# A graph attention layer: two conversions and a set of tables placed later in the prologue, and the last two steps and six pairs written out in a new order

## The chip, the cores and the metric

The kernel runs on one core of one Trainium2 chip. The time is device microseconds (us) of one execution. A core has engines that run their own instruction streams side by side: PE (matrix multiplies and transposes), DVE (vector work), ACT (scalar engine: copies, exponentials, gelu, square roots), POOL (GpSimd) and SP, which here only issues transfers. PEld in a profile is the loading of weights into PE. SBUF is the memory beside the engines, PSUM the small memory into which PE writes.

## The reference

One layer of graph attention with 12,500 nodes of 256 numbers, 8 heads of 32, and 200,000 edges, sorted by their destination `dst`:

```python
h = maximum(layernorm(x), 0)                       # 12500 x 256
q, k, v = h @ Wq + bq, h @ Wk + bk, h @ Wv + bv    # 8 heads of 32
logits = einsum(q[dst], k[src]) / sqrt(32)         # per edge and head
expv = exp(logits - segment_max(logits, dst)[dst])
attn = expv / segment_sum(expv, dst)[dst]
agg = segment_sum(attn * v[src], dst)              # per node
out = gelu(agg + h @ Wskip + bskip)
y = h + out
return x + layernorm(y) * gamma + beta
```

So each edge fetches a row of k and v of its source node, meets the q of its destination node, and is added into that node.

## The kernel before, in words

**Prologue.** `project()` (L156 to L279) walks the nodes in 98 blocks of 128, in groups of 1, 2, 4, then sixteen of 5, then 4, 4, 2 and 1. Per group `prepare` loads x (SP), takes the statistics (DVE L211 to L222) and writes h (ACT L226). Per block PE transposes h (L140), multiplies it by the weights of k and v (L257, three PSUM buffers `ps_kv`) and of q (L263, one PSUM buffer `ps_q`). DVE evicts both with their biases (kvo L260, qp L267); ACT L268 and POOL L269 split q into two parts. SP stores h, k and v, and q into tables in DRAM (`h_tab`, `kv_tab`, `q_pc`).

`make_plan` (L422 on) shares the prologue with it: it makes from the edge list what the walk needs. It loads dst and src (POOL), writes them out shifted (`dst_p`, `src_p`), gathers from these 66 rows per stream by 16 indirect transfers on POOL (`dch`, `sch`, L488), converts them to floats on DVE (`sf` L492, `df` L507), sends the first destinations through DRAM into one row (`d_d` L518, `d_row` L519; in the code they are called d0_d and d0_row), copies these (L523, L524, L552), transposes `sf` on PE (L496) into the gather indices `idx`, and ends with the tables `e_tab` (POOL L667) and a flag (L700). `make_near` (L703 to L758) makes tables of bands from POOL's masks: `near_m` L711 is written by POOL, DVE makes `near_p`, `near_s` (L740), `near_g`. In `project` it is called at group 4, and the small tables of biases (`pieces`, L112), gamma, the skip weights and a block of zeros for `q_pc` at group 3.

The order of instructions on each engine in this part is chosen by a scheduler that follows the dependencies and the order of the code. `behind` adds a dependency without a semaphore, which pins an instruction after another in the order of its engine. So a DVE conversion may stand ahead of the eviction of a later block, and then that eviction starts after it.

**Walk.** `walk_streams` (L760 on) cuts the edges into 8 streams and walks them in NST = 66 steps of 384 edges per stream, in 3 tiles of 128 (K = 3; the last step has 2). Per step POOL gathers 24 tiles of k and v by indirect DMA (L1035); PE spreads q over the edges (L1075), DVE multiplies (`times` L1084) and sums over the heads' elements (`total` L1091), PE turns the logits (`turn` L1099), DVE scans for running maxima (`maxima` L1110, L1111), ACT takes exponentials (L1117), PE turns the weights back (`turn_back` L1126), DVE weighs the values (`weigh` L1139), PE adds them up by node (`add_up` L1165), ACT copies the sums (L1177, L1183), and SP stores them into a table of partial sums (L1187). Here `keep` (L778) pins every instruction behind the one before on its engine: the order of calls in the code is the order on each engine.

**Pairs.** When all edges of two blocks of nodes are done, a `Pair` (L809) finishes them: `fetch` (sums, x and h by SP, L837), `divisors`, `divide` (L842 to L856, DVE), `turn` (transposes L850, copy hT on ACT L853), `skip` (h by the skip weights, L863, L867) and `add` (L872) on PE, `gelu` (ACT L876), `stats` (L879 to L885), `root` (ACT L889), `factors` (L893, L894), `normal` (ACT L899), `shifted` (x plus beta on PE, L906, L909), `scale` (L913, L915), `store` (SP L920). The function `table_of` (L987) loads an ACT table where the next function needs another. In the loop three pairs are in flight, called pair, before and older. The last four pairs are of the class `Last` (L923), which keeps its tiles in a half of a gathered k and v tile that is free.

**The end.** The loop runs to step 64; in its last round it takes in the pairs that are left. Step 65, its pair and the four `Last` pairs are then written out after the loop (the part from `c = NST - 1` on). Stores to `out` are at addresses known only at run time, and each waits for the one before.

Of the kernel before, what the change touches and what calls it, by code (L numbers as in the profile page):

```python
# [36 lines left out]
SP = mybir.EngineType.SP  # L37
DVE = mybir.EngineType.DVE
# [3 lines left out]
P = 128  # L42
# [28 lines left out]
def gnn_kernel(ctx: ExitStack, tc: tile.TileContext, x, src, dst, Wq, bq, Wk, bk, Wv, bv,  # L71
# [84 lines left out]
    def project():  # L156


        last, turned, products = None, None, []
# [9 lines left out]
        with tc.tile_pool(name="proj_c", bufs=1) as cpool, \  # L169
# [63 lines left out]
            for g, (b0, n) in enumerate(zip(starts, sizes)):  # L233
# [3 lines left out]
                if g == 4:  # L237
                    make_near(tc, near, near_n, lambda ins: behind(ins, last))
                if g == 3:
# [13 lines left out]
                for b in range(n):  # L253
# [13 lines left out]
                    nc.vector.tensor_tensor(q, ps_q, b_q, op=OP.add)  # L267
# [11 lines left out]
        return products  # L279
# [62 lines left out]
    with tc.tile_pool(name="pln", bufs=1) as pool, tc.tile_pool(name="pln_e", bufs=1) as ep, \  # L342
            tc.tile_pool(name="pln_ps", bufs=1, space=PSUM) as psum:
        products = project()
        make_plan(tc, pool, ep, psum, src, dst, N, LEN, NST, SLACK, NT, dram, ident, flag,
                  idx, d0_row, slot_row, e_tab, pen_tab, products, 4 * HID, 4 * KV)
# [75 lines left out]
def make_plan(tc, pool, ep, psum, src, dst, N, LEN, NST, SLACK, NT, dram, ident, flag, idx, d0_row,  # L422
              slot_row, e_tab, pen_tab, products, bytes_x, bytes_row):
# [6 lines left out]
    C = -(-max(E, (S - 1) * LEN + SLACK + STEP * NST + 1) // P)  # L430
    dst_p = dram.tile([1 + P * C, 1], I32, name="dst_p")
# [60 lines left out]
    nc.vector.tensor_copy(sf[:, :, :CH], sch)  # L492
# [14 lines left out]
    nc.vector.tensor_copy(df[:, :, :CH], dch[:, :, :CH])  # L507
# [15 lines left out]
    nc.vector.tensor_copy(line[:, 0, :], d0_row[:, :S])  # L523
    nc.vector.tensor_copy(line[:, 1, :], d0_row[:, (NST - 1) * S:])  # L524
# [27 lines left out]
    nc.vector.tensor_copy(done[:, :F - S], d0_row[:, S:])  # L552
# [207 lines left out]
def walk_streams(tc, N, HID, NST, KL, many, ident, idx, d0_row, slot_row, near, near_n, e_tab, pen_tab, h_tab,  # L760
# [26 lines left out]
    def loaded(a, most):  # L787

        return nc.values_load_multi_w_load_instructions(
            a, engines=[SP], min_val=0, max_val=most,  # L790
# [18 lines left out]
    class Pair:  # L809
# [36 lines left out]
        def turn(self):  # L846
# [5 lines left out]
            self.hT = self.pool.tile([P, 2, KC, P], F32, name="hT", bufs=1)  # L852
            self.keep(nc.scalar.copy(self.hT, ps))  # L853

# [67 lines left out]

    class Last(Pair):  # L923

        own, depth = "_l", 4

        def __init__(self, pool, m, room, ps_h, ps_o, keep):
            Pair.__init__(self, pool, m, ps_h, ps_o, keep)
            self.room = room
# [23 lines left out]
    with ExitStack() as es:  # L953
# [193 lines left out]

        def add_up(c, i, tiles=range(K)):

            add_up_products(c, i, tiles)  # L1150
            if tiles[-1] == tiles_of(c) - 1:
                add_up_results(c, i)

        def add_up_products(c, i, tiles=range(K)):
            g = step[c]
            streams = [s for s in range(S) if where(s)[0] == i]
            if tiles[0] == 0:
# [4 lines left out]
            for j in tiles:  # L1162
                for s in streams:
# [3 lines left out]
                                          g["vw"][j][:, s, :], start=j == 0,  # L1167
                                          stop=j == tiles_of(c) - 1, skip_group_check=True))

        def add_up_results(c, i):  # L1170
# [3 lines left out]
            if i == 0:  # L1174
                g["sums"] = work.tile([P, 3, SUMS], F32, name="sums_w", bufs=1)
# [47 lines left out]
        assert len(rest) <= 4  # L1223
        lasts, banks = [], {}

        def room(i):
            if i % 2 == 0:
                room.tile = rows[NST % 2][i // 2].rearrange("p s d -> p (s d)")
            half = S * KV // 2
            return room.tile[:, i % 2 * half:i % 2 * half + half]  # L1230

        def bank(i):
            def get():
                if i % 2 == 0:
                    banks[i // 2] = qe_ps.tile([P, 2, 2, HID], F32, name="ps_qe")
                return banks[i // 2][:, i % 2]
            return get

        def last(i):
            if i < len(rest):  # L1240
                lasts.append(Last(fin, rest[i], room(i),
                                  lambda: hot_ps.tile([P, 2, KC, P], F32, name="ps_hot"),
                                  bank(i), keep))
                lasts[i].fetch_rows()

        pair = before = older = None
        for c in range(NST - 1):
# [82 lines left out]
            if c == NST - 2:  # L1330
                if before:
                    before.shifted()
                    before.scale()
                    before.store(0)
                    before.store(1)
                if pair_next:
                    pair_next.fetch()
                for i in range(4):
                    last(i)
# [8 lines left out]
            if c == NST - 2:  # L1348
                weigh(c, K - 1)
                add_up(c, 0, range(K - 1, K))  # L1350
                add_up(c, 1)
                if pair_next:
                    pair_next.turn()
                    pair_next.skip()
            if c == NST - 2:
                add_up(c, 2)
            older, before, pair = before if c < NST - 2 else None, pair, pair_next
# [3 lines left out]
        c = NST - 1  # L1361
        for j in range(tiles_of(c)):
            if tiles_of(c) == K and j < 2:
                times(c, K - 1, j)
            hot_n(c, j)
            if tiles_of(c) == K and j == 1:
                total(c, K - 1)
        if tiles_of(c) == K:
            turn(c, K - 1)
        maxima(c)  # L1370
        exponent(c)
        if before:
            before.stats()
        if pair:
            pair.divisors()
            pair.divide()
        turn_back(c)
        carried(c)
        if before:
            before.root()  # L1380
# [413 lines left out]
```

## Time and profile before

| | us |
|---|---|
| median of 3 runs | 2448.26 |
| lowest, highest | 2444.04, 2455.95 |
| the profiled execution | 2449.12 |
| its span, from the first to the last instruction | 2447.3 |
| PE busy | 1708.7 (70%) |
| DVE busy | 1999.8 (82%) |
| ACT busy | 1066.4 (44%) |
| POOL busy | 1658.1 (68%) |
| first gather of the walk | 359.12 |
| last gather of the walk | 2360.52 |

Some 1.8 us of the profiled execution lie outside its span. The granted clock of PE has a mean of 0.737 of full speed. Busy shares are means over the whole span. In a row of a group, "x1576 | 1521.3, 965 | 482.4" means 1576 instructions, 1521.3 us of busy time, 965 ns for one, and 482.4 us in which the engine stood idle just before them; behind the arrow stands what ended the wait. In a row of a timeline the first number is the start from the beginning of the span, the second the duration, and the bracket the idle time before it.

### The profile page before, as it was taken

How to read it: one execution, taken by the hardware profiler on the slowest of the kernel's cores; microseconds unless marked ns; L12 is line 12 of the kernel's file. 1: busy time of each engine (PE TensorE's matmuls, PEld its weight loads, DVE VectorE, ACT ScalarE, POOL GpSimd, SP SyncE). 2: the span in 40 equal slices, each digit the busy share in tenths (PEclk: the TensorE clock that was granted, in tenths of full speed). 3: DMA queues.
4: the chain of work that ended last, by engine and by line, in shares of the span. 5: the costliest groups of instructions: out<-in, count | busy, mean ns of one | idle time of the engine just before them, and what ended most of it. 6: DMA issues, size and time to landing. Idle time of an engine off the chain costs nothing.

```text
span 2447.3 us, 29473 instructions
## 1 busy us (share of the span) xinstructions
PE 1708.7 (70%) x7824; PEld 909.6 (37%) x7824; DVE 1999.8 (82%) x2461; ACT 1066.4 (44%) x2328; POOL 1658.1 (68%) x1745
## 2 busy tenths in 40 slices
PE   6879983555557767767777767676676777677765
PEld 3445542222223333333333334333333343343333
DVE  7866856777778898898888888888888988888884
ACT  3333321333334544554545444445444444445443
POOL 4342447777777777777777777777777777777740
PEclk9999995666667777776667676677677767767678
DMA  7656668888888988888888988899889888889862
GB/s 259 253 207 264 251 250 263 256 255 254 255 268 266 286 276 282 285 277 284 279 285 279 287 271 282 274 285 288 275 282 287 282 281 284 277 279 287 279 202 76
DMA packets 306128, 649.33 MB, mean 265 GB/s; under 512 B 52836, under 2 KB 192238, under 8 KB 300954
## 3 DMA queue, kind: packets, MB, share of 16 engines
q0 software_dynamic: 128768, 423.23, 55.7%
q1 hardware_dynamic: 176434, 223.46, 27.2%
q8 instruction: 64, 1.05, 0.2%
q10 hardware_dynamic: 748, 0.66, 0.1%
q14 instruction: 114, 0.93, 0.1%
HBM read 538.91 MB, written 108.23 MB: 264 GB/s over the span
## 4 chain that ended last, share of the span: by engine, by line
DMA 25%; PE 23%; DVE 19%; issue 12%; POOL 10%; ACT 8%; SPq 3%; DVEq 0%; another core or an unknown queue 0%; ACTq 0%; POOLq 0%
DMA kv<-kv_tab,idx 16%; POOL kv L1035 9%; PE ps_kv L257 5%; DVE kv L1084 5%; DMA h<-h_tab 4%; PE ps_a L867 4%; DVE vw L1139 3%; DVE L L1091 3%; PE ps_qe L1075 3%; PE ps_q L263 3%; PE ps_a L1165 2%; ACT L987 2%; PE ps_hot L909 2%; DMA out_dram<-o 2%; SPq L837 2%
## 5 line engine op out<-in xcount | busy, mean ns | idle before, releaser
L1035 POOL DMA_INDIRECT kv<-kv_tab,idx x1576 | 1521.3, 965 | 482.4 <-issue 342.6
L1084 DVE TENSOR_TENSOR kv<-ps_qe,kv 128x1024 f32<-128x1024 f32 x394 | 468.8, 1218 | 191.1 <-DMA kv<-kv_tab,idx 117.9
L1139 DVE TENSOR_TENSOR vw<-ps_x,kv 128x2048 f32<-128x2048 f32 x197 | 449.4, 2281 | 9.1 <-PE ps_x L1126 9.1
L1091 DVE TENSOR_REDUCE L<-kv 128x64 f32<-128x2048 f32 x197 | 450.4, 2286 | 6.9 <-DMA et<-e_tab 0.2
L1075 PE MATMUL ps_qe<-qw,to_e 64*128 64x256 f32 (+1 forms) x1576 | 312.6, 396 | 107.5 <-DVE kv L1084 102.6
L1054 ACT ACTIVATE to_e<-ps_hot,ones 128x384 fp32r<-128x384 f32 x396 | 210.4, 573 | 316.1 <-PE ps_hot L1052 308.0
L1075 PEld LDWEIGHTS ps_qe<-qw,to_e 64*128 64x128 f32 (+1 forms) x1576 | 223.8, 248 | 272.7 <-DVE kv L1084 168.4
L1165 PE MATMUL ps_a<-vw,to_n 128*32 128x264 f32 (+1 forms) x2344 | 280.3, 516 | 4.2 <-DVE vw L1146 3.7
L1177 ACT COPY sums_w<-ps_a 128x264 f32<-128x264 f32 x130 | 49.2, 378 | 498.3 <-PE ps_a L1165 439.7
L1099 PE MATMUL ps_x<-ident,L 128*64 128x128 f32 x197 | 73.1, 371 | 274.0 <-DVE vw L1146 205.2
L1052 PE MATMUL ps_hot<-et,near 48*128 48x384 bf16 x396 | 142.5, 420 | 136.5 <-ACT to_e L1054 131.8
L257 PE MATMUL ps_kv<-w_kv,hT 128*128 128x512 f32 x392 | 194.8, 619 | 15.3 <-ACT hT L142 14.2
L269 POOL TENSOR_TENSOR qp<-qp 128x256 fp32r<-128x256 f32 x98 | 88.4, 903 | 171.8 <-ACT qp L268 171.6
L867 PE MATMUL ps_a<-w_s,hT 128*128 128x256 f32 x368 | 171.9, 648 | 21.2 <-ACT hT L853 18.0
L1165 PEld LDWEIGHTS ps_a<-vw,to_n 128*32 128x32 f32 (+1 forms) x2344 | 99.3, 139 | 216.2 <-issue 174.4
L1099 PEld LDWEIGHTS ps_x<-ident,L 128*64 128x64 f32 x197 | 25.7, 130 | 362.7 <-DVE vw L1146 288.3
L1165 PE MATMUL ps_hot<-vw,to_n 128*64 128x264 f32 x808 | 144.8, 509 | 1.9 <-DVE o L915 1.1
L1183 ACT COPY kv<-ps_a 1x264 f32<-1x264 f32 x388 | 142.9, 368 | 6.3
L867 PEld LDWEIGHTS ps_a<-w_s,hT 128*128 128x128 f32 x368 | 115.6, 329 | 69.0 <-ACT hT L853 44.1
L987 ACT ACT_TABLE_LOAD x102 | 130.9, 1283 | 1.7
L1065 ACT ACTIVATE to_n<-ps_hot,ones 128x384 f32<-128x384 f32 x197 | 103.6, 578 | 53.7 <-PE ps_hot L1063 51.8
L263 PE MATMUL ps_q<-w_q,hT 128*128 128x256 f32 x392 | 106.1, 395 | 24.3 <-DVE qp L267 24.2
(278 smaller groups left out, 2103.2 us busy)
## 6 DMA issues: line engine op xcount, KB each, us to landing
qw<-q_pc SPq DMA_DIRECT2D x264, 128.0 KB
kv<-kv_tab,idx POOLq DMA_INDIRECT x1576
kv_tab<-kvo SPq DMA_DIRECT2D x16, 1280.0 KB
q_pc<-qp SPq DMA_DIRECT2D x16, 1280.0 KB
qw<-q_pc SPq DMA_DIRECT2D x264, 64.0 KB
table<-sums_w SPq DMA_DIRECT2D x264, 61.9 KB
pen<-pen_tab SPq DMA_DIRECT2D x66, 192.5 KB
sums<-table SPq DMA_DIRECT2D x92, 132.0 KB
```

The lines of the kernel that those rows point to most:

```text
L257: ins = nc.tensor.matmul(ps_kv, hT[:, c, :], w_kv[:, c, :], start=c == 0, stop=c == KC - 1)
L263: ins = nc.tensor.matmul(ps_q, hT[:, c, :], w_q[:, c, :], start=c == 0, stop=c == KC - 1)
L867: self.keep(nc.tensor.matmul(self.ps[:, b, :], self.hT[:, b, c, :], w_s[:, c, :], start=False, stop=False, skip_group_check=True))
L987: keep(nc.scalar.activation(dummy[:, 1:2], dummy[:, 0:1], function))
L1035: ins = keep(nc.gpsimd.indirect_dma_start(out=t[:, s, :], out_offset=None, in_=kv_tab[:, :], in_offset=bass.IndirectOffsetOnAxis(ap=idx[:, ...
L1054: keep(nc.scalar.activation(step[c]["to_e"][:, i, :], ps[:, :CH], AF.Relu, scale=-1.0, bias=ones))
L1075: keep(nc.tensor.matmul(ps[:, b, a, :], g["to_e"][at:at + w, i, j * P:(j + 1) * P], g["qw"][at:at + w, i, :], start=True, stop=True))
L1084: keep(nc.vector.tensor_tensor(k, g["qe", half].rearrange("p b a d -> p a b d"), k, op=OP.mult))
L1091: keep(nc.vector.tensor_reduce(g["L"][:, j, :].rearrange("p (s h) -> p s h", s=S), g["kv"][j][:, :, :HID].rearrange("p s (h d) -> p s h d" ...
L1139: keep(nc.vector.tensor_tensor(t[:, :, HEADS:].rearrange("p s (h d) -> p s h d", h=HEADS), wj[:, :, :, None].to_broadcast([P, S, HEADS, D] ...
L1165: keep(nc.tensor.matmul(ps[at:at + w, :], g["to_n"][:, j, i * P + at:i * P + at + w], g["vw"][j][:, s, :], start=j == 0, stop=j == tiles_o ...
L1183: keep(nc.scalar.copy(step[c + 1]["kv"][0][0:1, s, HID - HEADS:], ps[at:at + 1, :]))
```

## The change

There are two parts.

In the prologue, `make_near` is called at group 13 instead of 4, and the small tables, gamma, the skip weights and the zeros at group 12 instead of 3. `project` now also returns the list of evictions of q (`biased`), and `make_plan` pins `df` behind the eviction at 36% of this list, `sf` behind that at 43%, and the copies of `d0_row` behind that at 45%.

At the end, the loop stops two steps earlier than the edge list, and the steps a = 64 and b = 65 are written out together. The add-ups of these two steps take the tiles in the order 1, 0, 2 (`turns`). The sums of b are copied into a free half of a gathered tile. The pair of step 64 (`late`) becomes a `Last`, so that there are five of them, and its rows and those of the others are fetched earlier. Three pairs, before, pair and late, are finished together as `ends`; their six stores are issued by POOL (`store_aside`) instead of SP. The four last pairs follow; their turn and skip are spread among the work of the others.

```diff
-                if g == 4:
+                if g == (4 if len(sizes) < 16 else 13):
                     make_near(tc, near, near_n, lambda ins: behind(ins, last))
-                if g == 3:
+                if g == (3 if len(sizes) < 16 else 12):
                     for ins in [rows(gam, gamma)] + \
                             [weights(w_s, Wskip)]:
                         behind(ins, products[-1])
...
-                    nc.vector.tensor_tensor(q, ps_q, b_q, op=OP.add)
+                    biased.append(nc.vector.tensor_tensor(q, ps_q, b_q, op=OP.add))
...
+    def behind(ins, share):
+
+        tc.add_manual_dep(ins.ins, biased[len(biased) * share // 100].ins.name,
+                          mybir.DependencyInfo(mybir.DependencyClass.NoSync,
+                                               mybir.DependencyReason.DATA), reason="kept order")
...
-    nc.vector.tensor_copy(sf[:, :, :CH], sch)
+    behind(nc.vector.tensor_copy(sf[:, :, :CH], sch), 43)
...
-    nc.vector.tensor_copy(df[:, :, :CH], dch[:, :, :CH])
+    behind(nc.vector.tensor_copy(df[:, :, :CH], dch[:, :, :CH]), 36)
...
-    nc.vector.tensor_copy(line[:, 0, :], d0_row[:, :S])
-    nc.vector.tensor_copy(line[:, 1, :], d0_row[:, (NST - 1) * S:])
+    behind(nc.vector.tensor_copy(line[:, 0, :], d0_row[:, :S]), 45)
+    behind(nc.vector.tensor_copy(line[:, 1, :], d0_row[:, (NST - 1) * S:]), 45)
...
-    nc.vector.tensor_copy(done[:, :F - S], d0_row[:, S:])
+    behind(nc.vector.tensor_copy(done[:, :F - S], d0_row[:, S:]), 45)
...
+        def store_aside(self):
+
+            nodes = loaded(slot_row[0:1, self.m, 0:2], (N - P) * BX, POOL)
+            for b in range(2):
+                self.keep(nc.gpsimd.dma_start(at_byte(out_b, nodes[b], P, HID),
+                                              self.y[:, b, :].bitcast(U8)))
...
+        def turns(c):
+
+            return range(K) if c < NST - 2 else (1, 0, 2)[:tiles_of(c)]
...
-        for c in range(NST - 1):
+        for c in range(NST - 2):
...
+        a, b = NST - 2, NST - 1
...
+        weigh(a, 0)
+        lasts[3].fetch_rows()
+        late.turn()
+        late.skip()
+        weigh(a, 2)
+        maxima(b)
+        add_up_products(a, 0, (0,))
+        add_up_products(a, 1, (1, 0))
+        exponent(b)
+        before.stats()
+        add_up(a, 0, (2,))
+        add_up_products(a, 2, (1, 0))
+        turn_back(b)
+        add_up(a, 1, (2,))
+        add_up(a, 2, (2,))
+        carried(b)
+        for j in range(2):
+            hot_n(b, j)
+        lasts[0].turn()
+        lasts[0].skip()
+        weigh(b, 1)
+        pair.divisors()
+        pair.divide()
+        pair.add()
         for i in range(3):
-            add_up(c, i, range(tiles_of(c) - 1))
-        weigh(c, tiles_of(c) - 1)
+            add_up_products(b, i, (1,))
+        table_of(AF.Gelu)
+        pair.gelu()
+        weigh(b, 0)
         for i in range(3):
-            add_up(c, i, range(tiles_of(c) - 1, tiles_of(c)))
...
+            add_up(b, i, (0,))
         for p in lasts:
             p.fetch_sums()
...
+        late.divisors()
+        late.divide()
+        late.add()
+        late.gelu()
+        pair.stats()
+        lasts[1].turn()
+        lasts[1].skip()
+        late.stats()
+        table_of(AF.Sqrt)
+        ends = (before, pair, late)
+        for p in ends:
+            p.root()
+        for p in ends:
+            p.factors()
+        for p in ends:
+            p.normal()
+        lasts[2].turn()
+        lasts[2].skip()
+        for i, p in enumerate(ends):
+            p.shifted()
+            p.scale()
+            p.store_aside()
+            if i == 0:
+                lasts[3].turn()
+                lasts[3].skip()
+            elif i == 1:
+                lasts[0].divisors()
+                lasts[0].divide()
+                lasts[0].add()
+        table_of(AF.Gelu)
+        for i, p in enumerate(lasts):
+            if i:
+                p.divisors()
+                p.divide()
+                p.add()
             p.gelu()
         table_of(AF.Sqrt)
```

## The prediction

> **What bounds the kernel now.** I read three things in this order: the page (what is busy, and when), the busy time by stretches of the span with the waits of the first stretch, and the single instructions where a wait looked long. The page first, its rows of 40 slices of 61 us each:
>
> ```profile
> span 2447.3 us, 29473 instructions
> ...
> DVE  7866856777778898898888888888888988888884
> ...
> POOL 4342447777777777777777777777777777777740
> PEclk9999995666667777776667676677677767767678
> ...
> L1035 POOL DMA_INDIRECT kv<-kv_tab,idx x1576 | 1521.3, 965 | 482.4 <-issue 342.6
> ```
>
> PEclk and POOL change character at slice 6 and at the last one: there are three stages, and they have different limits. The table by stretches (columns: PE, PEld, DVE, ACT, POOL busy, granted clock, DMA share, GB/s) shows how much each engine has to do in each:
>
> ```profile
> 60.00:80.00 20.00, 14.31 (x45) 7.36 (x44) 17.00 (x55) 3.49 (x10) 8.24 (x13) 0.98 0.31 132
> ...
> 100.00:120.00 20.00, 19.11 (x67) 11.28 (x66) 14.44 (x51) 9.14 (x24) 9.38 (x12) 1.00 0.90 321
> 120.00:140.00 20.00, 13.75 (x42) 7.75 (x41) 11.84 (x27) 5.16 (x14) 15.22 (x15) 0.91 0.56 216
> 140.00:160.00 20.00, 13.06 (x40) 7.47 (x39) 11.17 (x37) 5.21 (x14) 6.91 (x9) 0.83 0.57 209
> ...
> 200.00:240.00 40.00, 38.71 (x149) 24.01 (x149) 22.79 (x68) 15.14 (x42) 9.56 (x14) 1.00 0.64 243
> ...
> 357.00:2360.00 2003.00, 1353.43 (x6592) 703.86 (x6592) 1695.16 (x1696) 908.28 (x1945) 1520.78 (x1576) 0.69 0.88 276
> 2360.00:2447.00 87.00, 51.30 (x223) 30.11 (x223) 44.58 (x92) 33.61 (x65) 0.52 (x1) 0.77 0.31 94
> ```
>
> *The walk*, 357 to 2360: 1576 gathers on POOL, 0.965 us each plus 0.30 of "issue" between them, so 24 a step make 30.2 us, and the scans of successive steps do start 30 us apart (2289.80, 2319.62, 2350.29). The diff adds and removes no gather. This stage stays as it is, and whatever the first stage gains moves the end by as much.
>
> *The prologue*, 0 to 357: PE is busy 38.71 of 40 us where nothing disturbs it, and two blocks then take 6.16 us, 3.08 a block. The evictions of q (L267) date the blocks: block 0 at 19.5, 6 at 45.5, 18 at 92.1, 24 at 112.1, 36 at 163.8, 72 at 276.3, 78 at 299.8, 97 at 355.2. Against 3.08 a block, blocks 6 to 18 lose 46.6 - 37.0 = 9.6 us, 18 to 24 lose 1.5, 24 to 36 lose 51.7 - 37.0 = 14.7, 36 to 72 lose 1.6, 72 to 78 lose 5. The waits of this stage (us in total, times, longest) and two conversions in the order of time say who did it:
>
> ```profile
> PE ps_q L263 <- DVE qp L267: 24.2, 13, 6.6
> ...
> DVE st L211 <- DMA x_in<-in_x_dram: 10.0, 6, 4.3
> ...
> DVE near_s L740 <- POOL near_m L711: 5.0, 4, 2.1
> ```
>
> ```profile
> 131.39 1.94 DVE L507 CAST df<-dch 66x3072 f32<-66x3072 int32 x1 [5.96 <-DMA sch<-src_p,at_i]
> ...
> 151.22 1.76 DVE L492 CAST sf<-sch 66x3072 f32<-66x3072 int32 x1 [7.94 <-DMA sch<-src_p,at_i]
> ```
>
> DVE stands before a conversion whose gather has not landed, the eviction of the only ps_q buffer stands behind it in DVE's order, and PE waits 4.05 us at 134.31 and 6.56 us at 154.61, with 1.82 at 123.83 12.4 of its 24.2. Those two stretches are the ones with 13 to 14 us of PE in 20.
>
> *The tail*, 2360 to 2447: DVE is busy half of it. Its longest wait, and SP's at the very end:
>
> ```profile
> 2391.50 2.29 DVE L1139 TENSOR_TENSOR vw<-ps_x,kv 128x2048 f32<-128x2048 f32 x1 [9.10 <-PE ps_x L1126]
> ```
>
> ```profile
> SPq L920 <- DMA out_dram<-kv: 12.3, 7, 3.2
> ```
>
> **The change, part by part.** Times below are of the profiled execution, 2449.1 us with 1.8 around its span; the median of the runs shown is 0.9 lower.
>
> *1. Conversions later.* The two programs' instruction lists put df behind the eviction of block 36 (it was 29), sf behind 51 (was 33), the d0_row copies behind 52 (was 34). The gathers themselves are issued earlier, at blocks 14 to 21 instead of 25 to 31, because what fed them stood behind the tables on DVE. That leaves 15 blocks, 46 us, between the last gather and df; before, the last one landed by 151.2, about 35 us after the first was issued. So both waits (5.96 and 7.94) go, and with them PE's 12.4. DVE's work, counted by the times of its rows from start to start, in blocks 18 to 35 falls to 6 to 10 us per six blocks, against a pace of 18.5, so nothing is late next there. I take -12; bounds -12.4 and -6 (one of the two waits only, its share being given up elsewhere).
>
> *2. Loads of x.* The wait of 4.27 at 121.45 fell when the gathers crowded the DMA engines (0.90 busy from 100 to 120). The gathers move, so the crowd moves, to blocks where DVE has slack. I take -2; bounds 0 and -5.6 (4.27 and another 1.38 at 107.3).
>
> *3. Tables later.* make_near's 71 DVE instructions leave blocks 6 to 14 for 42 to 51. They are 25.6 us of busy time (some 18 from start to start, since successive ones overlap), with 5.0 of waiting for POOL's masks (near_s). At the old place blocks 6 to 18 lost 9.6; the counted work there falls from 19.2 and 19.1 us per six blocks to 17.4 and 15.8, under the pace: gain 5, between 0 and 9.6. At the new place it rises to 17.9, 18.9 and 20.1 in blocks 42 to 59, and the 5.0 of waits comes along: excess 0.4 + 1.6 = 2.0 at least, 9.6 at most (what the same tables cost at the old place); I take +5, between 7.0 (all of the waits) and 2.0. Parts 1 and 3 meet here: sf and the plan's chain behind it now stand at the tables' heels.
>
> *4. Other queues in the prologue.* ACT's two stores of zeros and its loads of gamma and the skip weights are issued 45 blocks later; nobody reads them before the walk, over 140 us on. On POOL, d_row waited 7.87 us for d_d, queued behind the gathers (below); POOL has that slack (it waits 171.6 for ACT at L269). The transposes of sf come two blocks later. The last e_tab row was issued at 324.6, 34 us before the first gather of the walk; two blocks later (6) with the end 14 nearer leaves 14 of cover. All this at nothing; if the plan came more than 14 us later than that, the walk would wait for it.
>
> Prologue: -12 - 2 - 5 + 5 = **-14**, bounds -6 + 9.6 = +3.6 and -12.4 - 5.6 - 9.6 + 2 = -25.6.
>
> *5. The last two steps.* The same pairs, products, copies and gathers as before, in another order on every engine, and three pairs' stores on POOL's queue. What it can remove is the 9.10 above: turn_back of step 65 stood on PE behind step 64's sums and a pair's skip, and is now put ahead of the sums that DVE does not wait for. What is late next: (a) DVE comes to the last products sooner, and they need the last gather, issued at 2359.57 and landed by 2364.1 whatever the order. DVE waited 0.20 there before; I take 2 (bounds 0 and the 4.5 from issue to landing). (b) The lasts' turn and skip move between the three finishing pairs. One pair's is 3.15 us (0.45 transposes, 0.59 the copy on ACT, 2.00 matmuls, gaps). One of them with its neighbour's copy on ACT ahead of what DVE wants costs about 4 (bounds 3.15 and two, 6.3). The b sums copied at 2400.7 then come some 7 earlier, their 8 loads too, which before began at 2405.11; but the three pairs' roots, factors, normals and scales now stand ahead of the lasts' divisions and gelus, where two of them were done while the sums travelled. Sum -9.1 + 2 + 4 = **-3**; bounds -9.1 + 3.15 = -6 and -9.1 + 4.5 + 6.3 = +1.7.
>
> *6. Stores on POOL's queue.* Every store to the output waits for the landing of the one before (the 12.3 above), so six on POOL run one by one and the lasts' eight on SP wait for the sixth. Ready: DVE's last weigh ended 2396.5, less 9.1 plus 2 is 2389.4; then divide 1.1, gelu 0.6, two stats 3.3, the table 1.5, factors 1.0, three normals 3.3, scale 1.4: 2402. The lasts' first store came at 2425.54, less 3 is 2422.5. So each of the six may take 20.5 / 6 = 3.4 us. Two rows of POOL stores with a reader behind them:
>
> ```profile
> 143.07 0.61 POOL L518 DMA_DIRECT2D d_d<-d_i  x1
> ...
> 152.32 0.75 POOL L519 DMA_DIRECT2D d_row<-d_d  x1 [7.87 <-DMA d_d<-d_i]
> ...
> 176.48 0.51 POOL L579 DMA_DIRECT2D gvu_d<-gvu  x1
> ...
> 178.46 0.58 POOL L581 DMA_DIRECT2D wide<-gvu_d  x1 [0.18 <-issue]
> ```
>
> The first took 9.2 us from issue to reader, right behind gathers that landed at 151.22; the second 2.0, with nothing ahead in its queue. In the tail the queue is empty for over 35 us: 2.0, so 12 us, done at 2414 and hidden. Taking SP's own issue away is worth nothing, since SP waits for landings.
>
> A rule on this: the Trainium skill ("DMA: Bandwidth & Descriptors", Anatomy of one DMA — SWDGE) fits 2.0 us plus the bytes over 436 GB/s to a transfer issued from this engine. For 128 KB that is 2.3, an estimate from that page; six end at 2416, which leaves the sum as it is.
>
> **Sum**: 2449.1 - 14 - 3 = 2432.
>
> **The rivals.** *A: the tables only change place.* DVE is the bound in blocks 42 to 59; they lose 9.6 there, the gain at the old place is 5, only one conversion's 6 is won and nothing on x. -6 - 5 + 9.6 = -1.4, tail -3: 2445. For it: 60 to 80 shows PE at 14.31 under just this work, and three groups of 18 to 20 us in a row leave no room. Against: 200 to 240 has DVE at 22.79 of 40, half empty. *B: slower, by the stores on POOL.* Place: the six stores that the lasts' first store waits for. At 9.2 us each they take 55 and end at 2457, 34.7 behind 2422.5: 2432 + 34.7 = 2467. It decides from 3.4 us a store on, cancels all gain at 3.4 + 17/6 = 6.2 and is 12 us slower than before at 8.3. Against: the empty queue. *C: more than forecast.* Both ends of parts 1 to 3 on the good side and the whole 9.1 less 3: about 2449.1 - 25.6 - 6 = 2417. *D: it does not do what it says*: the work on DVE is the same (254 us in both, counted by the rows' times from start to start), and the gaps return at other blocks: prologue 0, tail 0, 2449.
>
> **How the numbers follow.** Half a per cent, 12 us, is about what a measurement here can tell from no change. Forecast (2427 to 2436): 0.55. C: 0.11. A: 0.22. D: 0.04. B: 0.08. Faster 0.55 + 0.11 = 0.66, same 0.26, slower 0.08. The range goes from C's end, 2416, through A to D's edge, 2448, leaving out B and a little on each side; the forecast's own is 2424 to 2437.
>
> **What would show it.** Right: df and sf without a wait, PE busy over 18 of 20 us between blocks 20 and 40, the first gather of the walk near 345 instead of 359; the 9.10 gone and a wait for the last gather of about 2 in its place; the lasts' first store waiting for DVE, not for a store on POOL. Wrong: ps_q waiting for DVE in blocks 42 to 59 for more than 7 us (A); out_dram stores on POOL over 3.4 us apart (B); a first gather at 355 or later; DVE waits on PE in the last 50 us that add up to over 9.

## The result, and the profile after

The changed kernel takes 2431.14 us (median of 6, 2427.34 to 2435.5), the kernel before 2448.48 (median of 6 beside it). The ratio is 0.9931, 95% interval 0.9917 to 0.9945: 17 us, or 0.7%, faster. The forecast was 2432.

The page of the run after, 2429.78 us long with a span of 2428.1:

```profile
span 2428.1 us, 29469 instructions
...
L1058 POOL DMA_INDIRECT kv<-kv_tab,idx x1576 | 1517.3, 963 | 482.6 <-issue 339.2
```

The gathers (now L1058) are what they were. Stage by stage, with the start of the first and of the last gather as the borders (2360.52 in the table of the kernel before is where the last one ends):

| us | before | after | difference |
|---|---|---|---|
| start to first gather | 359.1 | 338.4 | -20.8 |
| first to last gather | 2000.5 | 1996.3 | -4.2 |
| last gather to the end of the span | 87.7 | 93.4 | +5.6 |

Four later runs at this speed have 2000.4 to 2004.4 in the second line, so its 4 us are what a walk differs by from run to run. The prologue gave more than forecast (-14), and the end took time in this run where it was to give 3.

The table by stretches (PE, PEld, DVE, ACT, POOL busy, granted clock, DMA share, GB/s), the same ones as before, and one more of the prologue:

```profile
60.00:80.00 20.00, 18.81 (x64) 10.62 (x63) 16.24 (x56) 7.12 (x20) 12.28 (x14) 1.00 0.98 358
100.00:120.00 20.00, 19.01 (x64) 11.07 (x65) 10.53 (x34) 8.53 (x25) 5.08 (x7) 1.00 0.67 252
120.00:140.00 20.00, 19.11 (x67) 11.49 (x66) 11.50 (x28) 8.31 (x22) 5.13 (x6) 1.00 0.79 281
140.00:160.00 20.00, 19.11 (x64) 10.75 (x62) 16.08 (x51) 6.82 (x18) 10.35 (x10) 1.00 0.62 234
180.00:200.00 20.00, 16.98 (x59) 10.04 (x58) 20.00 (x63) 6.47 (x17) 7.57 (x8) 0.91 0.47 172
2334.00:2428.00 94.00, 60.84 (x223) 34.65 (x223) 46.08 (x97) 28.90 (x61) 4.71 (x8) 0.67 0.29 94
```

PE is busy 19 of 20 us between 100 and 160, where from 120 on it had 13 to 14. From 180 to 200, where the tables now lie, DVE is busy 20.00 of 20 and PE falls to 16.98. In the last line PE's busy time is 60.84 where it was 51.30, with the same 223 instructions and a lower clock (0.67, it was 0.77).

The two conversions in the order of time have no wait behind them, and the waits of the prologue are these (us in total, times, longest):

```profile
136.87 1.72 DVE L515 CAST df<-dch 66x3072 f32<-66x3072 int32 x1
...
191.15 1.72 DVE L500 CAST sf<-sch 66x3072 f32<-66x3072 int32 x1
```

```profile
DVE st L212 <- DMA x_in<-in_x_dram: 10.4, 8, 2.1
PE ps_q L264 <- DVE qp L268: 8.2, 8, 2.7
...
DVE near_s L748 <- POOL near_m L719: 1.7, 3, 0.9
POOL d_row L527 <- DMA d_d<-d_i: 1.6, 1, 1.6
```

PE's wait for DVE at the one buffer of q fell from 24.2 us to 8.2. The wait for x has nearly the same sum as before (10.4 for 10.0), in smaller pieces and at other blocks: in blocks 18 to 36 it fell from 5.7 us to 0.8. The end, on DVE:

```profile
2339.87 1.23 DVE L1107 TENSOR_TENSOR kv<-ps_qe,kv 128x1024 f32<-128x1024 f32 x1 [2.83 <-DMA kv<-kv_tab,idx]
...
2355.28 2.29 DVE L1162 TENSOR_TENSOR vw<-ps_x,kv 128x2048 f32<-128x2048 f32 x1 [2.69 <-PE ps_x L1149]
...
2383.24 0.69 DVE L926 TENSOR_TENSOR o<-sums,ps_hot 128x512 f32<-128x512 f32 x1 [7.84 <-PE ps_hot L920]
...
2387.78 0.69 DVE L926 TENSOR_TENSOR o<-sums,ps_hot 128x512 f32<-128x512 f32 x1 [3.25 <-PE ps_hot L920]
...
2394.27 0.69 DVE L926 TENSOR_TENSOR kv<-kv,ps_hot 128x512 f32<-128x512 f32 x1 [4.11 <-PE ps_hot L920]
```

The 9.10 before the weigh of step 65 (L1162) is 2.69. DVE waits 2.83 for the last gather. New are three waits of `scale` for the x plus beta of its pair (L920), 15.2 us together. On PE, L920 of the first pair stands behind the third last pair's skip (L878), and that skip behind a copy on ACT:

```profile
2373.59 2.07 ACT L910 ACTIVATE sums<-sums,nm,rstd 128x256 f32<-128x256 f32 x4
2375.57 1.07 ACT L910 ACTIVATE kv<-kv,nm_l,rstd_l 128x256 f32<-128x256 f32 x2
2376.55 0.56 ACT L861 COPY hT<-ps_hot 128x512 f32<-128x512 f32 x1
```

```profile
2377.16 3.78 PE L878 MATMUL ps_qe<-w_s,hT 128*128 128x256 f32 x8 [2.90 <-ACT hT L861]
```

ACT works through six normals (L910) before it copies hT; PE waits 2.90 us for it and then runs the eight products in 3.78 us, which is half clock: the trace grants 0.50 from 2377.2 to 2381, and the same eight take 1.99 elsewhere. L920 of the second pair stands behind the next skip. L920 of the third stands behind no skip, but behind the `add` of the first last pair (L883), which waits for DVE's division:

```profile
2384.37 1.99 PE L878 MATMUL ps_qe<-w_s,hT 128*128 128x256 f32 x8 [0.41 <-ACT hT L861]
...
2389.62 2.07 PE L883 MATMUL ps_qe<-kv,ident 128*128 128x256 f32 x4 [1.88 <-DVE kv L867]
...
2392.16 2.08 PE L920 MATMUL ps_hot<-kv,ident 128*128 128x256 f32 x4
```

### The profile page after: what moved, and what is told of

It reads as the page before. It is cut to its first block, busy times and chain, and to the rows that moved or that the text cites. A ratio compares the mean times of both kernels' runs of the same rounds, so it can differ in the third digit from the quotient of the medians.

```text
span 2428.1 us, 29469 instructions
## 1 busy us (share of the span) xinstructions
PE 1697.2 (70%) x7824; PEld 904.4 (37%) x7824; DVE 1996.9 (82%) x2461; ACT 1061.4 (44%) x2323; POOL 1664.4 (69%) x1751
## 4 chain that ended last, share of the span: by engine, by line
DMA 27%; PE 22%; DVE 18%; issue 12%; POOL 11%; ACT 7%; SPq 3%; DVEq 0%; another core or an unknown queue 0%; POOLq 0%; ACTq 0%
DMA kv<-kv_tab,idx 18%; POOL kv L1058 10%; PE ps_kv L258 5%; DVE kv L1107 4%; DVE vw L1162 4%; PE ps_a L878 4%; DVE L L1114 4%; PE ps_q L264 3%; DMA h<-h_tab 3%; PE ps_qe L1098 2%; DMA out_dram<-o 2%; PE ps_a L1192 1%; DMA sums<-table 1%; PE ps_hot L920 1%; SPq L845 1%
## 5 line engine op out<-in xcount | busy, mean ns | idle before, releaser
L1058 POOL DMA_INDIRECT kv<-kv_tab,idx x1576 | 1517.3, 963 | 482.6 <-issue 339.2
L1162 DVE TENSOR_TENSOR vw<-ps_x,kv 128x2048 f32<-128x2048 f32 x197 | 449.4, 2281 | 3.6 <-PE ps_x L1149 2.7
L270 POOL TENSOR_TENSOR qp<-qp 128x256 fp32r<-128x256 f32 x98 | 96.3, 983 | 154.7 <-ACT qp L269 154.4
L878 PE MATMUL ps_a<-w_s,hT 128*128 128x256 f32 x352 | 164.6, 648 | 19.5 <-ACT hT L861 16.7
L1122 PEld LDWEIGHTS ps_x<-ident,L 128*64 128x64 f32 x197 | 24.7, 126 | 374.6 <-DVE vw L1169 300.6
L1192 PE MATMUL ps_hot<-vw,to_n 128*64 128x264 f32 x808 | 139.4, 494 | 0.0
L878 PEld LDWEIGHTS ps_a<-w_s,hT 128*128 128x128 f32 x352 | 110.5, 329 | 65.7 <-ACT hT L861 41.8
```

Source lines behind the costliest of these rows:

```text
L878: self.keep(nc.tensor.matmul(self.ps[:, b, :], self.hT[:, b, c, :], w_s[:, c, :], start=False, stop=False, skip_group_check=True))
L1058: ins = keep(nc.gpsimd.indirect_dma_start(out=t[:, s, :], out_offset=None, in_=kv_tab[:, :], in_offset=bass.IndirectOffsetOnAxis(ap=idx[:, ...
L1162: keep(nc.vector.tensor_tensor(t[:, :, HEADS:].rearrange("p s (h d) -> p s h d", h=HEADS), wj[:, :, :, None].to_broadcast([P, S, HEADS, D] ...
L1192: keep(nc.tensor.matmul(ps[at:at + w, :], g["to_n"][:, j, i * P + at:i * P + at + w], g["vw"][j][:, s, :], start=j == turns(c)[0], stop=j ...
```

## The experiments

All runs give two readings. One is the time from the start of one eviction of q to another, which dates the blocks; it repeats within 1.6 us between runs of the same order, except in blocks 0 to 6, which take 20.8 to 26.8 in kernels whose order there is the same or nearly so. The 3.5 us that the change seems to give there (26.1 to 22.6) are therefore not its own: its second run has 26.1.

| us in blocks | 0-6 | 6-18 | 18-36 | 36-42 | 42-60 | 60-97 | first gather at |
|---|---|---|---|---|---|---|---|
| before | 26.1 | 46.6 | 71.7 | 18.9 | 56.1 | 116.3 | 359.1 |
| both parts | 22.6 | 38.6 | 55.5 | 19.2 | 62.2 | 116.4 | 338.4 |
| both parts, again | 26.1 | 38.2 | 55.8 | 19.0 | 61.8 | 116.3 | 341.1 |
| prologue's part alone | 26.7 | 37.8 | 55.5 | 19.2 | 61.7 | 116.1 | 341.2 |
| the end's part alone | 25.9 | 46.5 | 70.1 | 18.3 | 56.2 | 116.4 | 357.0 |
| pins alone | 26.1 | 46.6 | 58.2 | 17.7 | 56.3 | 116.3 | 344.4 |
| tables later alone | 23.1 | 40.0 | 68.4 | 19.6 | 62.3 | 116.7 | 353.7 |
| tables at group 8 | 20.8 | 42.8 | 65.2 | 18.2 | 57.4 | 116.6 | 344.6 |
| tables at group 10 | 20.8 | 41.6 | 64.8 | 19.6 | 58.9 | 113.6 | 342.7 |
| two buffers of q | 26.8 | 38.2 | 55.2 | 18.5 | 63.7 | 117.3 | 343.7 |

Four runs are left out of this table: the prologue's part alone a second time, x plus beta ahead (twice) and its version with the stores on SP. Their prologue is that of both parts, and their first gathers come at 337.3 to 339.3.

The other reading is the end, with the 256-wide scans of step 65 as a mark in it:

| us | last gather to scans | scans to end | last gather to end |
|---|---|---|---|
| before | 17.1 | 70.6 | 87.7 |
| both parts | 14.4 | 79.0 | 93.4 |
| both parts, again (slower chip) | 26.2 | 72.5 | 98.7 |
| the end's part alone (slower chip) | 22.7 | 77.4 | 100.1 |
| prologue's part alone, first and second (slower chips) | 29.9, 30.6 | 71.3, 71.3 | 101.2, 101.9 |
| x plus beta ahead (slower chip) | 25.0 | 64.1 | 89.1 |
| x plus beta ahead, again | 13.4 | 65.8 | 79.2 |
| the same, stores on SP | 13.6 | 67.1 | 80.7 |

The first eight runs fell on chips on which the kernel before takes 2998.5 us (the first four) and 3007.5 (the next four); more on that at the end. The prologue and the durations of instructions are the same there; the walk is longer, and DVE lags behind POOL at its end, so that "last gather to scans" is only compared within a speed. The scans are a mark in the order of the work, and the new order moves work across it: DVE has 13.89 us of work ahead of them and 31.12 behind in the kernel before, 10.57 and 34.77 with both parts. So 3 to 4 us of what the two middle columns differ by is the same work on the other side of the mark; the last column is free of that.

### The prologue's part alone, and the end's part alone

The first leaves the end as it was, the second the prologue.

> The prologue's part alone, the end as in the kernel before. Theory (from the two traces): the prologue gives 20.8 us (first gather of the walk at 338.4 instead of 359.1) and the new end costs 5.6 (93.4 us from the start of the last gather to the end of the span, 87.8 before). Then this kernel has its first gather near 338, 88 us after the last gather, and a median of about 2427, some 4 us better than both parts together. Rival, the prediction's sum: the end gives 3 us, and the prologue 14; then this kernel is near 2434, some 3 us worse than both together.

> The new end alone, the prologue as before. Theory: first gather at 359, 93 us from the last gather to the end, a median of 2448 + 5 = 2453, with PE waiting for a copy of ACT that stands behind six normals, and skip products at half clock (3.8 us for eight) after it. Rival, the prediction's: the end gives 3 us, 85 from the last gather, median 2445.

The prologue alone: 2988.42 against 2998.50, ratio 0.9951 (0.993 to 0.9972), first gather at 341.2. The end alone: 2998.41, ratio 0.9998 (0.9983 to 1.0013), first gather at 357.0. So the gain is the prologue's, and the new order of the end is worth nothing, to within 5 us: the -3 of the forecast lies inside the interval, the +5 of the first theory just outside. From the last gather to the end these two traces differ by 1.1 us (100.1 and 101.2), 7 us less ahead of the scans and 6 more behind; some 4 of either is DVE's work that moved across the mark (20.58 us ahead of it for 24.70, 34.79 behind it for 30.94).

### The two halves of the prologue's part

Both of these runs have the end of the kernel before. Pins alone (the old calls stay, the pins are new):

```diff
-                if g == (4 if len(sizes) < 16 else 13):
+                if g == 4:
...
-                if g == (3 if len(sizes) < 16 else 12):
+                if g == 3:
```

> Only the pins on df, sf and the copies of d0_row, with the tables at their old place; gathers again at blocks 25 to 31, df behind block 36, sf behind 42. Theory: the waits of df and sf and the 14.7 us of blocks 24 to 36 go, the 11.5 that blocks 0 to 18 lose beside the tables stay, and blocks 42 to 60 don't lose the 6; first gather near 359 - 14 = 345, median about 2434. Rival, that what counts is the earlier gathers and not where the conversions stand: sf and df still wait, first gather at 355 or later, 2444.

The waits of the prologue in this run:

```profile
PE ps_q L263 <- DVE qp L267: 12.2, 11, 2.6
...
DVE near_s L747 <- POOL near_m L718: 5.0, 4, 2.1
```

df and sf are gone from the list, ps_q fell by 12.0 (from 24.2), and blocks 18 to 36 from 71.7 to 58.2. The first gather is at 344.4, where 345 was expected; median 2992.36, ratio 0.9983 (0.9968 to 0.9997).

Tables later alone (the new calls, no pins):

```diff
-    behind(nc.vector.tensor_copy(sf[:, :, :CH], sch), 43)
+    nc.vector.tensor_copy(sf[:, :, :CH], sch)
...
-    behind(nc.vector.tensor_copy(df[:, :, :CH], dch[:, :, :CH]), 36)
+    nc.vector.tensor_copy(df[:, :, :CH], dch[:, :, :CH])
...
-    behind(nc.vector.tensor_copy(line[:, 0, :], d0_row[:, :S]), 45)
+    nc.vector.tensor_copy(line[:, 0, :], d0_row[:, :S])
...
```

> Only the tables and loads later, no pins; the gathers go to blocks 14 to 20, and df (block 19) and sf (block 22) stand close behind them again. Theory: df and sf wait as before, some 6 and 8 us, at another block, blocks 0 to 18 give 8 to 11, the tables at blocks 42 to 51 cost 2 to 5 without the plan's chain behind them; first gather near 359 - 7 = 352, median about 2441. Rival, that the earlier gathers alone do it: first gather at 340.

The two conversions of this run:

```profile
87.69 1.76 DVE L514 CAST df<-dch 66x3072 f32<-66x3072 int32 x1 [4.52 <-DMA sch<-src_p,at_i]
...
105.52 1.76 DVE L499 CAST sf<-sch 66x3072 f32<-66x3072 int32 x1 [6.64 <-DMA d_d<-d_i]
```

The gathers came early and the conversions stood close behind them again: 4.52 and 6.64 us of waiting (the second is put down to d_d, whose transfer stands behind the gathers in POOL's queue). Blocks 18 to 36 take 68.4, and PE waits 19.4 us at ps_q. Blocks 42 to 60 take 62.3, some 6 us more than before, where 2 to 5 were expected. First gather 353.7, where 352 was expected; median 2997.31, ratio 0.9986 (0.997 to 1.0002). Earlier gathers alone don't do it; the distance between gather and conversion does, and the pins make it.

On this chip the medians of both halves moved by less than the first gather did (6 us of 13, 1 of 3, counted from the end's part alone, whose first gather is at 357.0). For the pins the interval, 1 to 10 us, leaves out the 13: here the earlier first gather did not reach the end in full. The walks of the four profiled runs there differ by 19 us (2534 to 2553), and no more can be said of it.

### The end: x plus beta ahead of the skips

```diff
+        before.shifted()
         for p in ends:
             p.root()
...
-        lasts[2].turn()
-        lasts[2].skip()
+        pair.shifted()
         for i, p in enumerate(ends):
-            p.shifted()
+            if i == 2:
+                p.shifted()
             p.scale()
             p.store_aside()
             if i == 0:
-                lasts[3].turn()
-                lasts[3].skip()
+                lasts[2].turn()
+                lasts[2].skip()
...
+        lasts[3].turn()
+        lasts[3].skip()
         table_of(AF.Gelu)
```

> Both parts, and in the new end the x-plus-beta products of the pairs before and pair are put ahead of the lasts' turns and skips on PE (late's behind the third one's skip, the fourth's turn and skip last). Theory: what the new end lost are DVE's waits for these products (7.84, 3.25 and 4.11 us in the run after the change), which stand on PE behind skips that wait for a copy queued behind six normals on ACT and then run at half clock. The first two of these waits shrink to under 1 us, the skip behind them takes 2.0 instead of 3.8, and from the 256-wide scans of step 65 to the end of the span it takes 70 us or less instead of 79; the median falls 8 to 10 us below that of both parts. Rival: DVE's wait moves to the next product and the stores on POOL become what the last stores wait for; under 3 us gained.

Beside it on the same chip ran both parts as they are, and the prologue's part alone:

> Both parts as they are, on the same chip as its neighbours, as their yardstick. First gather 17 to 21 us earlier than before; 77 to 79 us from the 256-wide scans of step 65 to the end.

> The prologue's part alone, beside both parts on one chip. Theory: the new end is 6 to 8 us longer from the 256-wide scans of step 65 on, and 3 to 7 shorter ahead of them, so the two kernels lie within 6 us of each other, this one ahead where POOL's issue bounds the walk. Rival, the prediction's: both parts are 3 us ahead.

Medians beside 3007.52 before: x plus beta ahead 2978.21 (ratio 0.9900, 0.9881 to 0.9918), both parts 2984.32 (0.9922, 0.9901 to 0.9943), prologue alone 2983.27 (0.9932, 0.9911 to 0.9954). Both parts and the prologue alone are again the same. From the scans to the end both parts took 72.5 here, where 77 to 79 were expected, the prologue alone 71.3, and x plus beta ahead 64.1. Its median is 6.1 us below that of both parts, where 8 to 10 were expected, and the two intervals overlap; from the last gather to the end it took 89.1 instead of 98.7. A second run of x plus beta ahead, in a later set, has on DVE:

```profile
2378.95 0.69 DVE L926 TENSOR_TENSOR o<-sums,ps_hot 128x512 f32<-128x512 f32 x1
...
2380.34 0.69 DVE L926 TENSOR_TENSOR o<-sums,ps_hot 128x512 f32<-128x512 f32 x1
...
2385.35 0.69 DVE L926 TENSOR_TENSOR kv<-kv,ps_hot 128x512 f32<-128x512 f32 x1 [2.62 <-PE ps_hot L920]
```

The first two waits are gone, so the order on PE made them; that is shown. The third, whose product still stands behind L883, is 2.62.

The clock is another matter. In the second run of both parts the skip waited as long and then ran at full clock:

```profile
2938.66 1.99 PE L878 MATMUL ps_qe<-w_s,hT 128*128 128x256 f32 x8 [2.91 <-ACT hT L861]
```

So the half clock in the first run is not fixed by the wait before it. With it the three waits of DVE were 7.84, 3.25 and 4.11; without, 5.17, 3.25 and 2.00. So 4.8 of the 6.5 us between the two runs (79.0 and 72.5) lie in these waits and came with the lower clock. Another 2.0 is DVE's wait before the weigh of step 65 (2.69, and 0.69 in the second run); that it has to do with the clock is not shown.

### Where the tables stand

```diff
-                if g == (4 if len(sizes) < 16 else 13):
+                if g == (4 if len(sizes) < 16 else 8):
```

> Both parts, but make_near is called at group 8 instead of 13, so its DVE work lies at blocks 18 to 27, where DVE has 6 to 10 us of work per six blocks, and no longer at 42 to 51. Theory: the 6.1 us that blocks 42 to 60 lost go, at most 1 to 2 come in at blocks 18 to 30; first gather of the walk 4 to 5 us earlier than with both parts as they are. Rival: the waits for POOL's masks stop PE wherever the tables stand; nothing gained.

First gather 344.6, later and not earlier (both parts on that chip: 341.1); median 2990.38, ratio 0.9940 (0.9914 to 0.9967). Blocks 42 to 60 did fall to 57.4, but 18 to 36 rose from 55.5 to 65.2. One wait of DVE there:

```profile
90.34 0.42 DVE L748 TENSOR_TENSOR near_s<-near_m 48x256 f32<-48x256 f32 x1 [3.99 <-POOL near_m L719]
```

POOL was issuing the gathers of the edge lists, 0.95 us each, and the first mask stood behind them. So the tables were put behind the gathers, at group 10, in the version with x plus beta ahead:

> The new order of the end with x plus beta ahead, and make_near at group 10: its DVE work at blocks 28 to 37, behind the last of the 16 gathers on POOL (block 19), where at group 8 the masks stood behind these gathers and DVE waited 3.99 us for one. Theory: with POOL free the tables cost nothing in the slack of blocks 24 to 37 (at most 2 us), blocks 42 to 60 lose 1 to 2 instead of 6; blocks 18 to 60 take 131 to 133 us instead of 136.5. Rival: the waits for the masks are as dear there as anywhere; 18 to 60 takes 136 or more.

Median 2426.44 (2446.62 before on that chip), ratio 0.9918 (0.9905 to 0.9932). Blocks 18 to 60 take 143.3, where the rival said 136 or more: without the collision the tables still cost 9 us in blocks 18 to 36. The masks were not free there either: DVE waits 4.1 us for them, after 5.2 at group 8 and 1.7 at group 13. And the room was gone once the tables stood in it: DVE is busy 16.20 of 21.33 us in blocks 24 to 30 and 21.81 of 24.98 in blocks 30 to 36, where it is busy 10.53 and 8.59 of 18.5 with both parts. Two more runs of that set:

```diff
-            p.store_aside()
+            p.store(0)
+            p.store(1)
```

> The new order of the end with x plus beta ahead, and the six stores of the three pairs issued by SP instead of POOL. Theory: a store waits for the landing of the one before on either queue; SP's own stores were 1.8 to 2.2 us apart, POOL's 2.3 to 3.1, so SP is done 1 to 4 us sooner; with SP waiting only 0.6 us for DVE in the run before, that is worth 0 to 1 us at the end. Rival, that POOL's queue was of use because SP is busy with loads: 3 us slower or more from the 256-wide scans on.

> The new order of the end with x plus beta ahead, as it was, as the yardstick of its two neighbours; 64 to 70 us from the 256-wide scans of step 65 to the end, blocks 18 to 60 of the prologue 136 to 137 us.

Stores on SP: 2422.44, ratio 0.9908 (0.9892 to 0.9923). On POOL: 2421.89, ratio 0.9901 (0.9886 to 0.9916). The two can't be told apart, so the queue from which these six are issued makes no difference here, to within some 4 us. They are the fastest versions of this study, 24.2 and 24.7 us below the kernel before beside them, where both parts had 17.3. The edit of the second is the one under x plus beta ahead.

The last run gave PE a second buffer for q, at the price of one for k and v:

```diff
-                    ps_kv = psum.tile([P, 2 * HID], F32, name="ps_kv", bufs=3)
+                    ps_kv = psum.tile([P, 2 * HID], F32, name="ps_kv", bufs=2)
...
-                    ps_q = psum.tile([P, HID], F32, name="ps_q", bufs=1)
+                    ps_q = psum.tile([P, HID], F32, name="ps_q", bufs=2)
```

> The new order of the end with x plus beta ahead, and in the projection two PSUM buffers for q and two for k and v (one and three before), so that PE can run one product of q further ahead of DVE. Theory: what the tables cost wherever they stand (6 us at blocks 42 to 54, 9 to 10 at 18 to 36, though DVE has room there on the mean) is that a burst of them between two evictions stops PE at the one buffer of q; with two, blocks 42 to 54 take 40 us or less instead of 43.3, and the first gather of the walk comes 3 to 5 us earlier, near 334. Rival: over these blocks DVE is simply full, or kept up by POOL's masks; 43 us again.

Median 2434.08 (2451.65 before on that chip), ratio 0.9928 (0.9915 to 0.9942). Blocks 42 to 54 take 44.2, no better than 43.3, and the first gather comes at 343.7 and not near 334. PE's waits for DVE at ps_q are gone in blocks 42 to 60 (4.6 us with both parts), and the time is the same, so the theory of the single buffer falls for this place. DVE is busy 21.60 of 21.65 us in blocks 48 to 54, as it is 20.00 of 20 in the stretch from 180 to 200 above. That k and v have a buffer less here could hide a gain; this was not taken apart. For blocks 18 to 36 two buffers weren't tried, and how much of the 9 us there is DVE's work and how much the masks stays open.

## Why the prediction was right

The forecast was 2432 and 2431.14 came, in its range, with the sign and the stage as told. That it came so close is luck: the prologue gave some 4 us more than forecast and the end some 3 less, and the two errors cancel. By its parts:

**Conversions later and loads of x (parts 1 and 2), -12 and -2.** Blocks 18 to 36 gave 16.2, and the pins alone 13.5. ps_q's wait fell by 12.0 in the run with the pins alone, against the 12.4 that the forecast read from the trace. Right. The wait for x did not shrink in sum; as the forecast had it, it moved. In blocks 18 to 36 it fell from 5.7 us to 0.8, and with the pins alone, where the gathers stay, it is 6.3; the 2.7 us between 16.2 and 13.5 fit the forecast's 2, but no run has this part alone.

**Tables later (part 3), -5 and +5.** Blocks 6 to 18 gave 8.0 (5 was taken between 0 and 9.6), blocks 42 to 60 cost 6.1 (5 between 2 and 7). Right in kind, the gain taken too small. The forecast's counted work per six blocks pointed at the right place: blocks 42 to 54 rose from 37.6 to 44.1 us. The price was near partly by luck: the excess of 2.0 and the 1.7 us that DVE waited for the masks, of the 5.0 that were to come along, make 3.7 of the 6.1. Nor is the count a rule: it says that blocks 18 to 36 have room, and there the tables cost 9 to 10. Rival A, that the tables only change place, was the right fear with the wrong price: they did cost as forecast for it in blocks 18 to 36, not in 42 to 60. Its sign, more than 7 us of waiting at ps_q in blocks 42 to 59, did not come (4.6).

**Other queues (part 4), nothing.** From the last eviction to the first gather it took 3.9 us before and 4.2 after. Right.

**The last two steps (part 5), -3.** Wrong, by 3 us if the run of the end alone is taken (nothing, with -3 inside its interval) and by 9 in the first trace (+5.6), and hidden by the prologue's surplus. From the last gather to the end the traces of the slower chips are nearer to it: 100.1 for 101.2 on one, 98.7 for 101.9 on the other. (a) The wait for the last gather, taken as 2, was 2.83; the 9.10 became 2.69 rather than nothing. (b) The step that failed is the price of "about 4, bounds 3.15 and 6.3" for turns and skips between the three finishing pairs. It was 15.2 in the first run and 10.4 (5.17 + 3.25 + 2.00) in the second. The forecast counted one pair's turn and skip, once. What it left out is the queue of ACT, where the copy that PE needs stood behind six normals, and that each of three pairs has an x plus beta to wait for: the first two stood behind a skip, the third behind the `add` of the first last pair, so a price was paid three times. With two of the three put ahead the time from the scans to the end fell from 72.5 to 64.1. The forecast's own sign, DVE waiting for PE for more than 9 us in the last 50, came with 15.6. That the end took no more than it did has a reason that the forecast did not price: DVE's waits for anything but PE and the last gather fell from some 16 us to 11 between the last gather and the end, while those for PE rose from 9.5 to 19.2.

**Stores on POOL (part 6), nothing.** The first two in the run after, in the order of time on POOL, and two of the waits of SP in the end (us in total, times, longest; the last pairs' own stores, 17.5 us in all, are left out):

```profile
2384.60 0.61 POOL L938 DMA_DIRECT2D out_dram<-o  x1 [48.90 <-issue]
2386.94 0.56 POOL L938 DMA_DIRECT2D out_dram<-o  x1 [1.73 <-DMA out_dram<-o]
```

```profile
SPq L931 <- DMA out_dram<-o: 15.6, 1, 15.6
SPq L931 <- DVE kv L926: 7.1, 1, 7.1
```

A store took 2.34 us to the next, near the 2.0 taken from gvu_d and far from the 9.2 of d_d; SP had passed the last of them and then waited 7.1 us for DVE. Rival B, from 3.4 us a store on, was not in force. The fit of the Trainium skill ("DMA: Bandwidth & Descriptors", Anatomy of one DMA — SWDGE), 2.3 us for 128 KB by the estimate in the forecast, agrees with 2.34, 2.25 and 2.27 measured between the two stores of each pair. It is no upper bound: with x plus beta ahead the first pair's two were 3.12 us apart in one run and 3.86 in the other.

So the sum came out for two reasons: the prologue gave 17.8 (8.0 + 16.2 - 6.1 - 0.3) for the forecast's 14, and the end nothing for its 3.

## What to carry to other kernels

An operation that waits for a transfer costs what stands behind it in its engine's order, so put distance between an issue and its consumer, and pin the consumer, for a scheduler that follows the code's order will pull it up again. Mean slack of an engine over a stretch does not say that work fits there; the same tables cost 6 us where DVE was nearly full and 9 to 10 where it had been half empty until they came. When a hand-written order interleaves two chains, price it on every engine that the chains cross: here a copy on ACT behind six others set what PE and then DVE waited for.

## What the runs showed of the hardware

The same kernel before took 2447 to 2452 us in three sets of runs and 2998 and 3008 in two others, on other chips, with the same prologue (first gather at 357.0 in the end's part alone there, at 359.1 here) and the same durations (a gather's issue 0.95 to 0.96 us). The difference is the walk: 2534 to 2553 us on the longer ones. The stretch of the walk in the prologue's part alone, there:

```profile
357.00:2885.00 2528.00, 1485.46 (x6504) 763.97 (x6508) 1677.51 (x1677) 904.51 (x1916) 1502.40 (x1563) 0.63 0.71 216
```

The DMA engines moved 216 GB/s with 0.71 of their time, where the kernel before had 276 and 0.88. Over the whole stretch that is nearly the same DMA time, 1795 us for 1763. POOL no longer issued without a pause: 529 us of its waits, 116 in number, are put down to DVE, which had a buffer still in use. What held DVE up is not shown. Of the chain of work that ended last 4% is DMA there, for 25% before; 24% is "issue" and 11% has a releaser that the profile does not know. So it is open whether the transfers took longer or the engines that use them. A change in a stage's fixed work can be read on either; the ratio can't be carried over.

The granted clock after a PE wait differed between two runs of one program: 0.50 for 3.8 us after a wait of 2.90, and 1.00 after a wait of 2.91 at the same place. The `add` behind the wait of 1.88 us (L883) took 2.07 in the first of these runs and 1.13 in the second, behind a wait of the same length. The Trainium skill ("TensorE: Matmul & The Clock Gate", What's actually happening) says that the window in which activity is watched runs freely, so that a kernel's cold stretch differs from run to run; these rows fit that. Its rule against idle gaps over about 3.4 us (HAM oscillation — how this bites in real kernels) did not hold as a safe side here: 2.90 and 1.88 were each followed by half clock once.
